# The residual x plus the output's bias, made in DRAM by DMA instead of on GpSimd

## The chip, the core and the metric

The kernel runs on one NeuronCore of a Trainium2 chip. The core has five engines that run their own instruction streams: TensorE (PE; its weight loads are listed as PEld), VectorE (DVE), ScalarE (ACT), GpSimd (POOL) and SyncE (SP, which here only issues DMAs). They wait for each other by semaphores. DMAs issued by SP and by GpSimd run on the same 16 DMA engines; the profile calls SP's queue q1 and GpSimd's q0. SBUF is the memory on the core (128 partitions), PSUM the small memory that TensorE writes into, DRAM the memory off the core.

The metric is the device time of one execution in microseconds; the median of three runs is given.

## The reference

The input x has 4 batches of 1024 tokens with 512 channels, ctx the same shape. One layer of cross attention with 16 heads of 32 channels is followed by a quantised feed-forward net:

```python
x = x + xattn(layernorm(x), ctx, Wq, bq, Wk, bk, Wv, bv, Wo, bo)
x = x + ffn(layernorm(x), clip_x, clip_down, w_gate, w_up, w_down)

# xattn: q from layernorm(x); k and v from ctx
scores = q k^T / sqrt(32), masked:
    # the first 768 tokens, "image", attend within their own third of 256
    # the last 256, "text", attend to all image tokens and causally to text
out = softmax(scores) v @ Wo + bo

# ffn: activations fake-quantised to 8 bits with ONE scale for the whole tensor
xq = round(x / s) * s          # s = sigmoid(clip) * max|x| / 127
h  = fakequant(silu(xq @ Wg^T) * (xq @ Wu^T))
y  = h @ Wd^T
```

The scale s needs the maximum over all tokens, so the feed-forward part cannot begin before the attention is done with every token. The sum x + bo has nothing to do with the attention: it is one number for each element of x and could be made at any time before the attention's output is added to it.

## The kernel before

**Tiles and stages.** The 4096 tokens are cut into 16 blocks of 256; each batch has three image blocks and one text block. The attention stage takes about 880 us, the feed-forward stage the rest. Between them the sum x + attention lies in a DRAM tensor, x1_d (the profile leaves out digits in names and calls it x_d).

**Units.** One unit is a block and a group g of four heads against one key block. An image block has 4 units (its own key block only), a text block 16: four groups with four parts each, one part for each key block of its batch. That makes 112 units. The loop over n, of 118 iterations, runs a software pipeline: iteration n makes the row maxima of unit n (products s, then L450 or L468 on VectorE), the weights of unit n - 5 (T_LAG; products t of L504 and L509, exponentials L514 and L518 on ScalarE) and the values of unit n - 6 (V_LAG; products av, L554). Projections of q, k and v and the output's products (pp_q, pp_kv, pv, po, all at L226) fill TensorE in between, by a table of targets. An iteration takes 5 to 10 us.

**Row sums.** GpSimd adds the exponentials of a unit into sp (L535), twice for most parts of a text unit; in a text block's last part it also clears the upper triangle (L523). TensorE then sums sp by a product with ones (L573), in the values step one iteration later.

**The normalised input.** layernorm(x) of a block is made in three background steps, one for each iteration as they come up: statistics (VectorE, L365), deviation (two small operations on ScalarE, then seven on GpSimd, L373 to L379) and apply (ScalarE, L383). The normalised block goes to DRAM (xn_d) and comes back as spread_q in another order of rows; VectorE transposes it (L267) into the operand of the q projection. The tile xb that holds the block has one buffer, so the next xb is loaded when the write of xn_d has landed. The loads of ctx (spread_kv) take the same way and share spread_q's one buffer. The background is a queue: the deviation at its head holds back what stands behind it, the quantising of the feed-forward weights.

**The bias.** bo_b holds the bias of the output in all 128 partitions; in iterations 2 to 5 the part of bv that passes through Wo is added to it (output_bias; complete at L206).

**The output.** When a block's four groups are done, its xr, a 512 KB block of x, is loaded (L136, two buffers). GpSimd adds bo_b to it (add_bias, L613), one or two iterations after the load is issued. The product po of 128 tokens is added by VectorE (take, L618), which frees po's PSUM bank, the only one that the projections and the outputs share. Statistics for the second layernorm and the token's maximum and minimum follow (L625 to L628), and GpSimd issues the write of the block to x1_d (L631). The last block (tail) is added to its products by TensorE instead.

**What sets the order.** TensorE, VectorE, ScalarE and GpSimd run their instructions in the order in which the program writes them. SP is not in that list: the order of its DMA issues is made by a planner from what is ready when. An engine's instructions, SP's DMA issues too, start in order: one that waits holds up those behind it.

Of the kernel before, what the change touches and what calls it, by code (L numbers as in the profile page):

```python
# [10 lines left out]
F32 = mybir.dt.float32  # L11
# [3 lines left out]
ALU = mybir.AluOpType  # L15
# [4 lines left out]
P = 128  # L20
B, N, C = 4, 1024, 512
NH, D = 16, 32
FF = 1408
NCC = C // P
NIC = FF // P
QB = 256
NQB = N // QB
# [15 lines left out]
def kernel(ctx: ExitStack, tc: tile.TileContext, x, kv, Wq, bq, Wk, bk, Wv, bv, Wo, bo, clip_x, clip_down, w_gate, w_up, w_down, out):  # L43
    nc = tc.nc
    x_tok = x.rearrange("b n c -> (b n) c")
# [7 lines left out]
    x1_d = dram.tile([B * N, C], F32, tag="x1_d", name="x1_d")  # L53
# [68 lines left out]
    with ExitStack() as actx:  # L122
        wk2 = actx.enter_context(tc.tile_pool(name="wk2", bufs=2))
# [4 lines left out]
        ap = actx.enter_context(tc.tile_pool(name="ap", bufs=1))  # L128
# [5 lines left out]
        def load_block(src, c, tag, bufs=1):  # L134
            t = ld.tile([P, 2, C], F32, tag=tag, name=f"{tag}_{c}", bufs=bufs)
            nc.sync.dma_start(t, src[c * QB : (c + 1) * QB, :].rearrange("(t p) c -> p t c", p=P))  # L136
            return t
# [10 lines left out]

        brow = ap.tile([3 * NCC, P], F32, tag="brow", name="brow")
        bqk = ap.tile([P, 3 * NCC], F32, tag="bqk", name="bqk")  # L150
        bo_b = ap.tile([P, C], F32, tag="bo_b", name="bo_b")
        mask = ap.tile([P, P], F32, tag="mask", name="mask")
        NMB = 4
        nm2s = [ap.tile([P, 2, 4, D], BF16, tag=f"nm2_{i}", name=f"nm2_{i}") for i in range(NMB)]
# [18 lines left out]

        def other_loads():
            nc.sync.dma_start(W["Wo"], Wo.rearrange("(c p) f -> p c f", p=P))
            nc.gpsimd.dma_start(bo_b, bo.partition_broadcast(P))
            for name, clip in (("x", clip_x), ("h", clip_down)):
                sig[name] = cpool.tile([P, 1], F32, tag=f"sig_{name}", name=f"sig_{name}")
                nc.gpsimd.dma_start(sig[name], clip.partition_broadcast(P))
# [8 lines left out]
        def output_bias():  # L188

            bvr = wk2.tile([P, NCC, D], F32, tag="wst", name="bvr", bufs=1)  # L190
            parts = wk2.tile([P, C], F32, tag="sp", name="bo_parts")

            def spread():
                nc.vector.memset(bvr, 0.0)
                nc.vector.tensor_copy(bvr[:, :, 0:1], bqk[:, 2 * NCC :].unsqueeze(2))

            def product():
                pb = ps_sc.tile([P, 2, 2, QB], F32, tag="sc", name="pbo").rearrange("p a b c -> p a (b c)")[:, 0, :]
                for cc in range(NCC):
                    nc.tensor.matmul(pb[rows_of(cc)], bvr[:, cc, :], W["Wo"][:, cc, :], start=True, stop=True, tile_position=(0, cc * D), skip_group_check=True)  # L200
                nc.scalar.copy(parts, pb)

            def total():
                pb = ps_sc.tile([P, 2, 2, QB], F32, tag="sc", name="pbt").rearrange("p a b c -> p a (b c)")[:, 0, :]
                nc.tensor.matmul(pb, ones, parts, start=True, stop=True)
                nc.vector.tensor_tensor(bo_b, pb, bo_b, ALU.add)  # L206

            return spread, product, total

# [41 lines left out]
        class Job:  # L251


            def __init__(self, kind, c, a):
                self.kind, self.c, self.a = kind, c, a
                self.small, self.big, self.part = 0, 0, 0
                self.smalls = 2 if c == 0 else 1
                self.bigs = 4 if kind == "kv" else 2
# [93 lines left out]
        background = deque()  # L352
# [54 lines left out]
        def rows_of(j):  # L407
            return slice(j * D, (j + 1) * D)
# [181 lines left out]

                return avs, av, quotient

        at_end = [False]
        later = []

        class Output:


            def __init__(self, k):
                self.k, self.xr, self.i, self.part, self.biased = k, None, 0, 0, False  # L600

            def load(self):
                if self.xr is None:
                    self.xr = load_block(x_tok, self.k.c, "xr", bufs=2)
                    if at_end[0]:
                        later.append(self.add_bias)
                    else:
                        later.append(lambda: later.append(self.add_bias))

            def add_bias(self):  # L610
                if not self.biased:
                    self.biased = True
                    nc.gpsimd.tensor_tensor(self.xr, self.xr, bo_b.unsqueeze(1).to_broadcast([P, 2, C]), ALU.add)  # L613

            def take(self, po, i, cols):
                self.add_bias()
                xr, t0 = self.xr, 2 * self.k.c
                nc.vector.tensor_tensor(xr[:, i, cols], po[:, cols], xr[:, i, cols], ALU.add)  # L618
                if cols.stop < C:
                    return None  # L620
                name = f"st2_{self.k.n}_{i}"

                def statistics():
                    st = small.tile([P, 6], F32, tag="st2", name=name)
                    nc.vector.bn_stats(st, xr[:, i, :])  # L625
                    nc.vector.bn_aggr(mv2[:, t0 + i, :], st)
                    nc.vector.tensor_reduce(xm2[:, t0 + i, 0:1], xr[:, i, :], AX.X, ALU.max)
                    nc.vector.tensor_reduce(xm2[:, t0 + i, 1:2], xr[:, i, :], AX.X, ALU.min)  # L628

                if i == 1:  # L630
                    nc.gpsimd.dma_start(x1_d[t0 * P : (t0 + 2) * P, :].rearrange("(t p) c -> p t c", p=P), xr)  # L631
                return statistics
# [50 lines left out]
        T_LAG, V_LAG = 5, 6  # L683
        units = []
        for b in range(B):
            for qb in range(NQB) if b < B - 1 else (0, TEXT, 1, 2):
                k = Block(b, qb)
# [3 lines left out]
        LATE = len(units) - n_text - 3 * NCC  # L691
# [94 lines left out]
        def step_output(half=False, rests=False):  # L786
            rest = outputs[0].step(half)
            if outputs[0].i == 2:
                outputs.pop(0)

                def take():
                    rest[1]()
                    for o in outputs[:2]:
                        o.load()

                finish((rest[0], take), rests)
            else:
                finish(rest, rests)
# [57 lines left out]
        stage()  # L856
        stage()
        take()
        spent, rows_done["k", 0] = 2 * BIG, NCC
        stage()  # L860
# [9 lines left out]
        send(3)  # L870
        big_step()
        other_loads()
        early[0] = False
        spread, product, total = output_bias()
        for n in range(len(units) + V_LAG):
            at_end[0] = n >= len(units)
            previous = units[n - 1] if 0 < n <= len(units) else None
            if n < len(units):
                u = units[n]
# [6 lines left out]
                    minus_maxima(u)  # L886
            if n in (2, 3, 4, 5):
                (spread, sigmoids, product, total)[n - 2]()
            f = background.popleft() if background and n > 0 else None
            if f is not None and f.__name__ in ("deviation", "apply", "quantise"):  # L890
                f()
                f = background.popleft() if background and f.__name__ == "quantise" else None
# [100 lines left out]
        for i in range(2):  # L993
            t = t0 + i
# [27 lines left out]
    gctx = ExitStack()  # L1022
    f4 = gctx.enter_context(tc.tile_pool(name="f4", bufs=NTT))
    fd = gctx.enter_context(tc.tile_pool(name="fd", bufs=1))
    fd.tile([P, 56], F32, tag="pad", name="pad")

    fx = gctx.enter_context(tc.tile_pool(name="fx", bufs=2))
    xt = load_x1(fx, 0)
# [160 lines left out]
    def steps(h):  # L1189

        return h.rearrange("p i t -> p (i t)").bitcast(BF16).rearrange("p (i u) -> p i u", i=NIC)[:, :, :TB]
# [9 lines left out]
    for n, tb in enumerate(order):  # L1201
        hq, xr = steps(resident[tb]), xrs.pop(tb)
# [74 lines left out]
```

## Time and profile before

| | |
|---|---|
| median of 3 runs | 1130.96 us (1130.71 to 1133.3) |
| the profiled execution | 1132.25 us, of which the span from first to last instruction is 1130.5 us |
| granted TensorE clock, mean | 0.995 |
| TensorE busy | 1106.8 us (98%) |
| VectorE, GpSimd, ScalarE busy | 783.8, 549.0, 502.1 us |
| GpSimd: sums into sp (L535) | 84 and 59 operations, 188.2 and 140.2 us |
| GpSimd: bias adds (L613) | 16 operations, 38.1 us |
| GpSimd: issues of x1_d's writes (L631) | 15, 11.9 us |
| HBM read, written | 71.57 MB, 33.29 MB |

Times are microseconds from the start of the span unless a row says ns. A group's row gives the line, the engine, the operation, what it writes and reads, its shape and number; then busy us and mean ns of one; then how long its engine sat idle before it and what ended that. A row of waits reads "engine line <- whom it waited for: us in total, times, longest". SPq is SP's stream of DMA issues: the duration there is the issue, not the transfer. Matmuls are pipelined, so a busy TensorE need not be at its peak; idle time of an engine that is not the bottleneck costs nothing.

### The profile page before, as it was taken

The page shows a single profiled execution, that of the slowest core. Times are in us where ns is not written, and L with a number is a line of the kernel's source. Part 1 is how long each engine was busy: PE and PEld are TensorE (multiplying, and loading weights), DVE is VectorE, ACT ScalarE, POOL GpSimd, SP SyncE. Part 2 cuts the span into 40 slices and gives each one's busy share as a digit, 9 for nine tenths or more (in the row PEclk, how much of TensorE's full clock was granted, in tenths as well). Part 3 has the DMA queues.
Part 4 walks back from the last instruction along what each step waited for, and adds up shares of the span by engine and source line. Part 5 has one row for each costly group of instructions (what it writes and reads, how often), then busy time and mean ns, then how long its engine had stood idle before and what let it go on. Part 6 is the DMA issues. An engine that isn't in the chain of part 4 may idle for free.

```text
span 1130.5 us, 31464 instructions
## 1 busy us (share of the span) xinstructions
PE 1106.8 (98%) x13829; PEld 553.5 (49%) x13851; DVE 783.8 (69%) x980; ACT 502.1 (44%) x701; POOL 549.0 (49%) x616
## 2 busy tenths in 40 slices
PE   9999999999999999999999999999999899998998
PEld 5545545454445445454544445555544344443444
DVE  2546676766577857567777656876666788877887
ACT  3234444343444434344433345544342465553553
POOL 1224556677754576775646668668753232110110
PEclk9999999999999999999999999999999899999999
DMA  8342223132322231331323123112221599311895
GB/s 261 111 132 65 63 56 96 47 97 76 90 63 76 74 97 43 94 104 36 89 66 88 41 74 86 42 50 63 73 76 47 185 289 253 73 34 33 299 379 191
DMA packets 117201, 119.09 MB, mean 105 GB/s; under 512 B 55548, under 2 KB 86536, under 8 KB 115656
## 3 DMA queue, kind: packets, MB, share of 16 engines
q1 hardware_dynamic: 111104, 83.26, 26.7%
q0 software_dynamic: 5648, 33.30, 7.8%
q8 instruction: 108, 1.77, 0.7%
q10 hardware_dynamic: 312, 0.53, 0.2%
q14 instruction: 29, 0.24, 0.1%
HBM read 71.57 MB, written 33.29 MB: 93 GB/s over the span
## 4 chain that ended last, share of the span: by engine, by line
PE 84%; POOL 7%; DVE 3%; DMA 3%; ACT 2%; issue 1%; POOLq 0%; DVEq 0%; SPq 0%; ACTq 0%
PE pv L226 9%; PE pp_kv L226 8%; PE pp_q L226 8%; PE av L554 8%; PE po L226 8%; PE t L509 7%; PE pg L1117 7%; PE pu L1117 7%; PE s L457 5%; POOL sp L535 4%; PE s L446 4%; PE av L573 3%; PE t L504 3%; PE pd L1220 2%; DMA xt<-x_d 2%
## 5 line engine op out<-in xcount | busy, mean ns | idle before, releaser
L514 ACT ACTIVATE pT<-t 128x1024 f32<-128x1024 f32 x112 | 114.8, 1025 | 332.1 <-PE t L509 310.0
L535 POOL TENSOR_TENSOR sp<-sp,pT 128x1024 f32<-128x1024 f32 x84 | 188.2, 2240 | 45.0 <-ACT pT L518 41.6
L535 POOL TENSOR_TENSOR sp<-pT 128x1024 f32<-128x1024 f32 x59 | 140.2, 2376 | 97.7 <-ACT pT L518 86.7
L468 DVE TENSOR_REDUCE nmh<-s 128x2 f32<-128x1024 f32 (+1 forms) x128 | 145.2, 1157 | 60.1 <-PE s L457 57.9
L450 DVE TENSOR_REDUCE nmh<-s 128x4 f32<-128x1024 f32 x96 | 112.8, 1218 | 84.3 <-PE s L446 84.3
L226 PE MATMUL pv<-Wv_sb,kvT 128*32 128x512 f32 (+1 forms) x1088 | 120.5, 570 | 1.6 <-DVE xr L618 1.6
L226 PE MATMUL pp_q<-qT,Wq_sb 128*32 128x256 f32 x2048 | 121.3, 380 | 0.2
L554 PE MATMUL av<-pT,va 128*32 128x256 f32 (+1 forms) x1792 | 116.9, 377 | 0.0
L226 PE MATMUL po<-Wo_sb,oT 128*32 128x512 f32 (+1 forms) x1120 | 112.2, 534 | 2.7 <-DVE xr L618 2.4
L518 ACT ACTIVATE pT<-t 128x1024 f32<-128x1024 f32 x112 | 114.5, 1023 | 0.0
L509 PE MATMUL t<-qT,kT 32*128 32x256 f32 (+1 forms) x1792 | 113.4, 366 | 0.0
L226 PE MATMUL pp_kv<-kvT,Wk_sb 128*32 128x256 f32 x1920 | 112.5, 380 | 0.1
L588 DVE RECIPROCAL avs<-avs 128x256 f32<-128x256 f32 x63 | 109.7, 1742 | 0.0
L509 PEld LDWEIGHTS t<-qT,kT 32*128 32x128 f32 x1792 | 88.1, 184 | 6.7
L1117 PE MATMUL pg<-xqT,wgT 128*128 128x512 bf16 x344 | 90.0, 381 | 1.1 <-DVE xqT L1078 0.5
L1117 PE MATMUL pu<-xqT,wuT 128*128 128x512 bf16 x345 | 90.2, 382 | 0.4
L589 POOL TENSOR_TENSOR oT<-avs 128x256 f32<-128x256 f32 x63 | 46.2, 734 | 90.1 <-DVE avs L588 89.9
L1123 ACT ACTIVATE silu<-pg,sg 128x512 f32<-128x512 f32 x88 | 60.0, 687 | 65.3 <-PE pg L1117 63.2
L226 PEld LDWEIGHTS pp_q<-qT,Wq_sb 128*32 128x32 f32 x2048 | 63.3, 110 | 48.3 <-issue 5.5
L1144 DVE SCALAR_TENSOR_TENSOR h<-pu,su,silu 128x512 f32<-128x512 f32 x88 | 65.4, 747 | 30.5 <-PE pu L1117 27.8
L226 PEld LDWEIGHTS pp_kv<-kvT,Wk_sb 128*32 128x32 f32 x1920 | 60.2, 110 | 43.6 <-issue 2.3
L554 PEld LDWEIGHTS av<-pT,va 128*32 128x32 f32 x1792 | 47.0, 109 | 53.5 <-issue 30.0
(191 smaller groups left out, 1448.0 us busy)
## 6 DMA issues: line engine op xcount, KB each, us to landing
xt<-x_d SPq DMA_DIRECT2D x16, 1024.0 KB, 6.1
h<-h_d POOLq DMA_DIRECT2D x3, 2816.0 KB, 14.2
xb<-in_x_dram SPq DMA_DIRECT2D x16, 512.0 KB, 3.7
xr<-in_x_dram SPq DMA_DIRECT2D x16, 512.0 KB, 3.6
x_d<-xr POOLq DMA_DIRECT2D x16, 512.0 KB, 3.7
spread_kv<-in_ctx_dram SPq DMA_DIRECT2D x60, 128.0 KB, 2.8
xn_d<-xb SPq DMA_DIRECT2D x15, 512.0 KB, 3.4
spread_q<-xn_d SPq DMA_DIRECT2D x60, 128.0 KB, 2.7
```

Of the source, the lines that this page charges most:

```text
L226: nc.tensor.matmul(out[rows_of(j)], lhs[:, rows_of(j)], rhs, start=start, stop=stop, tile_position=(0, j * D), skip_group_check=True)
L450: nc.vector.tensor_reduce(nmh[:, h, :, :, 0], prs[h], AX.X, ALU.max, negate=True)
L468: nc.vector.tensor_reduce(nmh[:, h, :, i, half], s[:, :, :n], AX.X, ALU.max, negate=True)
L509: nc.tensor.matmul(prs[j // 2][:, j % 2, n, cols], kc[rows_of(j), g, n * P : (n + 1) * P], q[rows_of(j), g, cols], start=False, stop=(n == 1))
L514: nc.scalar.activation(pT[:, :2], prs[0], AF.Exp)
L518: nc.scalar.activation(pT[:, 2:], prs[1], AF.Exp)
L535: nc.gpsimd.tensor_tensor(sp[:, :, cols], a, pT[:, :, n, cols], ALU.add)
L554: nc.tensor.matmul(av[rows_of(j), 0, cols], va[:, n, g * P + j * D : g * P + (j + 1) * D], u.pT[:, j, n, cols], start=(u.part == 0 and n = ...
L588: nc.vector.reciprocal(avs[:, 1, :], avs[:, 1, :])
L1117: nc.tensor.matmul(ps, w[:, cc, ic * P : (ic + 1) * P], qT[:, cc, :], start=(cc == 0), stop=(cc == NCC - 1))
L1123: nc.scalar.activation(s, pg, AF.Silu, scale=sg[:, ic : ic + 1])
L1144: nc.vector.scalar_tensor_tensor(h[:, ic, :], pu, su[:, ic : ic + 1], s, ALU.mult, ALU.mult)
```

## The change

x + bo is made in DRAM, in x1_d itself, early in the attention stage. When bo_b is complete (iteration 5), SP issues four DMAs that write it to every row of x1_d, one DMA for each batch: 128 partitions, eight rows of 2 KB from each, 2 MB. In iterations 7 to 22 GpSimd issues one DMA each that adds 256 rows of x to the same rows of x1_d (a DMA from DRAM to DRAM that accumulates). The block xr is then loaded from x1_d instead of x, with three buffers instead of two, and GpSimd's adds are gone. bo_b itself is loaded by SP instead of GpSimd, and takes one of the three buffers of oT, which hold a block's attention output before Wo; a pad in the feed-forward stage grows by 2 KB for each partition, the difference between the larger xr and the smaller bo_b.

A second change is in the background: while the weights step is at the third or fourth part of a text unit (and before LATE, iteration 84), a deviation at the head of the queue stays there, and nothing is taken from the queue in that iteration.

```diff
-        bo_b = ap.tile([P, C], F32, tag="bo_b", name="bo_b")
+        bo_b = wk2.tile([P, NCC, QB], F32, tag="oT", name="bo_b", bufs=3).rearrange("p a b -> p (a b)")[:, :C]
...
-            nc.gpsimd.dma_start(bo_b, bo.partition_broadcast(P))
+            nc.sync.dma_start(bo_b, bo.partition_broadcast(P))
...
                 nc.vector.tensor_tensor(bo_b, pb, bo_b, ALU.add)
+                for b in range(B):
+                    rows = x1_d[b * N : (b + 1) * N, :].rearrange("(t p) c -> p t c", p=P)
+                    nc.sync.dma_start(rows, bo_b.unsqueeze(1).to_broadcast([P, N // P, C]))
...
             def load(self):
                 if self.xr is None:
-                    self.xr = load_block(x_tok, self.k.c, "xr", bufs=2)
-                    if at_end[0]:
-                        later.append(self.add_bias)
-                    else:
-                        later.append(lambda: later.append(self.add_bias))
-
-            def add_bias(self):
-                if not self.biased:
-                    self.biased = True
-                    nc.gpsimd.tensor_tensor(self.xr, self.xr, bo_b.unsqueeze(1).to_broadcast([P, 2, C]), ALU.add)
+                    self.xr = load_block(x1_d, self.k.c, "xr", bufs=3)
 
             def take(self, po, i, cols):
-                self.add_bias()
                 xr, t0 = self.xr, 2 * self.k.c
...
-            f = background.popleft() if background and n > 0 else None
+            if 7 <= n < 7 + B * NQB:
+                rows = slice((n - 7) * QB, (n - 6) * QB)
+                nc.gpsimd.dma_start(x1_d[rows, :], x_tok[rows, :], accum_op=ALU.add, max_dma_last_dim=C)
+            t = units[n - T_LAG] if T_LAG <= n < LATE else None
+            crowded = t is not None and t.k.text and t.part > 1
+            f = background.popleft() if background and n > 0 and not (crowded and background[0].__name__ == "deviation") else None
...
-    fd.tile([P, 56], F32, tag="pad", name="pad")
+    fd.tile([P, 568], F32, tag="pad", name="pad")
```

More of the change, by code (lines that the diff above doesn't have):

```diff
@@ L591, in values @@
                 return avs, av, quotient
-        at_end = [False]
         later = []
@@ L599, in __init__ @@
             def __init__(self, k):
-                self.k, self.xr, self.i, self.part, self.biased = k, None, 0, 0, False
+                self.k, self.xr, self.i, self.part = k, None, 0, 0
             def load(self):
                 if self.xr is None:
-                    self.xr = load_block(x_tok, self.k.c, "xr", bufs=2)
-                    if at_end[0]:
-                        later.append(self.add_bias)
-                    else:
-                        later.append(lambda: later.append(self.add_bias))
-            def add_bias(self):
-                if not self.biased:
-                    self.biased = True
-                    nc.gpsimd.tensor_tensor(self.xr, self.xr, bo_b.unsqueeze(1).to_broadcast([P, 2, C]), ALU.add)
+                    self.xr = load_block(x1_d, self.k.c, "xr", bufs=3)
             def take(self, po, i, cols):
-                self.add_bias()
                 xr, t0 = self.xr, 2 * self.k.c
@@ L875 @@
         for n in range(len(units) + V_LAG):
-            at_end[0] = n >= len(units)
             previous = units[n - 1] if 0 < n <= len(units) else None
```

## The prediction

> **What bounds the kernel now.** I read the page first, then what TensorE waits for, then the two stretches that the change touches: the first 110 us of the attention loop, and the text groups with the loop's end.
>
> ```profile
> PE 1106.8 (98%) x13829; PEld 553.5 (49%) x13851; DVE 783.8 (69%) x980; ACT 502.1 (44%) x701; POOL 549.0 (49%) x616
> ```
>
> TensorE is busy for 98% of 1130.5 us, so it is the bound. POOL, which the change relieves, is busy for 49%. What POOL's work costs is only what TensorE waits for. The list of TensorE's own waits (total us, times, longest) says how much that is:
>
> ```profile
> PE av L573 <- POOL sp L535: 2.6, 7, 0.7
> PE po L226 <- DVE xr L618: 2.4, 2, 1.8
> ...
> PE pv L226 <- DVE xr L618: 1.6, 2, 0.8
> ```
>
> The last two are the output path: L618 adds a product to xr and frees the only projection bank. The list of all waits puts L618's own lateness on POOL ("DVE xr L618 <- POOL xr L613: 18.0, 4, 6.1"): four times the bias add came late, and TensorE lost 4.0 us. That is all that the bias costs now.
>
> **Part 1: the bias add leaves POOL.** Two groups of the by-form listing price it:
>
> ```profile
> L613 POOL TENSOR_TENSOR xr<-xr,bo_b 128x1024 f32<-128x1024 f32 x16 | 38.1, 2378 | 5.4 <-DMA xr<-in_x_dram 5.3
> ...
> L631 POOL DMA_DIRECT2D x_d<-xr x15 | 11.9, 791 | 16.5 <-DVE xr L618 16.2 <-issue 0.2
> ```
>
> 16 adds of 2378 ns go, 38.1 us of POOL. 16 accumulating DMAs come, issued by POOL. The trace has none; the nearest row is L631, 791 ns to issue 512 KB. From below, the 541 ns of the h_d writes; from above, twice L631, as both sides are rows in DRAM. I take 791: 12.7 us, so POOL is relieved of 25 us. Of that only the waits count. At 305 and 518 us the late add held the next pv by 0.8 us each; at 837 by 0.6; at 855 the add waits for its load, issued at 852.14 because the second xr buffer was in use until L628 at 852.08, and po waits 1.8. The third buffer lets that load go early. Gain **4.0 us**, the sum of the two rows.
>
> **Part 2: factors out of the last text parts.** The factors are seven small POOL operations, 1.8 us from 284.99 to 286.79. They move only where they meet a text unit's third or fourth part; by the times of L373 those at 285, 498 and 648 us do. At 285 the triangle select that follows could have started at 286.2, when the exponentials ended, and starts at 286.75: 0.5 us of the 0.7 us wait at the row-sum product. Twice, as 648 meets no wait behind it: **1.0 us**. The price is a normalised block an iteration or two later (6.7 us each). Its cover is that the load of spread_q at 677.96 waits for a DVE transpose anyway; without cover that block would cost up to 6 us.
>
> **Part 3: the bias written to DRAM through SP's queue.** This is where the time is lost. Once bo_b is complete, four DMAs of 2 MiB each write it to all 4096 rows of x1_d. In time order around there (start, us, engine, operation):
>
> ```profile
> 70.18 0.67 DVE L206 TENSOR_TENSOR bo_b<-pbt,bo_b 128x512 f32<-128x512 f32 x1
> ...
> 75.57 0.38 SPq L385 DMA_DIRECT2D xn_d<-xb  x1
> ...
> 78.37 0.39 SPq L136 DMA_DIRECT2D xb<-in_x_dram  x1
> ...
> 80.21 1.93 SPq L146 DMA_DIRECT2D spread_q<-xn_d  x4
> ...
> 89.17 0.64 DVE L365 BATCH_NORM_STATS2 st<-xb 128x6 f32<-128x512 f32 x1
> ...
> 90.99 2.15 DVE L267 STREAM_TRANSPOSE qT<-spread_q 128x1024 f32<-128x1024 f32 x1 [0.17 <-PE pp_q L226]
> ...
> 93.08 2.31 DVE L450 TENSOR_REDUCE nmh<-s 128x4 f32<-128x1024 f32 x2
> ...
> 95.95 0.40 PE L504 MATMUL t<-nmT,onesb 2*128 2x512 bf16 x4
> ```
>
> The writes go out at 70.85, ahead of the write of xn_d. What follows on SP's queue then waits for their data: small transfers behind large ones on this queue show it. The DMA issues at 7.5 us (behind Wv and Wq) and at 896.5 us (behind a 1 MiB xt), with size and us to landing:
>
> ```profile
> spread_kv<-in_ctx_dram SPq DMA_DIRECT2D x1, 128.0 KB, 10.2
> ...
> xqT<-xq SPq DMA_TRANSPOSE x1, 5.5
> ```
>
> Alone these take 2.4 to 2.8 and 2.4 us. The rate comes from 1041.4 us, where four xt loads of 1 MiB stand on this queue:
>
> ```profile
> xt<-x_d SPq DMA_DIRECT2D x1, 1024.0 KB, 5.6
> ```
>
> The first lands after 5.6 us; while they run the slices show about 395 GB/s, 2.65 us per MiB, so 2.95 us is fixed. Eight MiB: 70.85 + 2.95 + 8 x 2.65 = **95.0 us**. The Trainium skill, "DMA: Bandwidth & Descriptors", section "Anatomy of one DMA", gives 2.0 us plus the bytes at 436 GB/s: 21.2 us, done at 92.1, which would make the stall below 2.9 us shorter. Our row has this queue and 2 KB packets, so I keep 95.0 and the other for the range.
>
> One accumulation is in the way too. POOL issues the first one after nm at 87.96, when the first 2 MiB are down (about 79), so POOL doesn't wait, but its data shares the engines with the end of the writes. By the row, 512 KB is 1.3 us. The Trainium skill, "Collectives: The Full Stack", section on the bandwidth ceiling, says that an adding DMA reads two sources and takes twice a copy's read traffic: an estimate of 2.65 us. No run here shows an accumulation; I take 2.65, with 0 and 5.3 as the ends. By the row alone the stall would be 1.3 us shorter.
>
> The chain from there, each step with its present duration: xn_d is 0.5 MiB, 1.3 us, landed at 95.0 + 2.65 + 1.3 = 99.0. xb cannot load before that (one buffer). From the issue of xb to the last spread_q landing it takes 86.1 - 78.4 = 7.8 us now: 106.8. The statistics of L365 wait in between, from 89.2 on, and VectorE does its work in order, so the transpose (2.15) and the maxima (first half 1.2) come behind: 110.2. The second bank of t's products is one that those maxima free; TensorE needs it at 96.2. **Stall: 14.0 us**, in the ninth iteration. Behind L365 on VectorE stand L267, L450 and L588, and POOL's nm waits for L450, but the stall at TensorE covers these. The transposes of nm behind the writes are used four iterations after their issue (88.7 is due at about 139), so they cost nothing.
>
> After some 3.6 us without products between 1042 and 1046 the granted clock was 0.5 for 3.4 us (0.68 in the window 1045 to 1050). The same after this hole costs half of 3.4: **1.7 us**.
>
> The other pieces cost nothing, by their cover: the 256 KB of bo on SP instead of POOL (0.7 us of queue at 13 us, where two xr loads of 512 KB leave the same queue; without that, 0.7 us); bo_b in one of three oT buffers (third block's oT, iteration 14, after 140 us; without cover, the wait for the writes); the pad (it keeps the later pools where they were); the loads of xr from DRAM rows that were summed long before (first used at 148.7). Accumulations 2 to 16 come one to an iteration of 7 to 10 us and fall on chains with 6 us of slack (spread_q issued at 116.71, its four parts landed by 121, used at 127.02). POOL's issues of iterations 18 to 22 meet text units; 0.8 us there could delay a row sum by as much, four times at most.
>
> **Sum.** -4.0 - 1.0 + 14.0 + 1.7 = +10.7 us. The profiled execution took 1132.25 us (span 1130.5 and 1.75 around it): 1142.95. The median shown is 1.3 lower: 1130.96 + 10.7, about **1141 us** with the small terms rounded down.
>
> **Rivals.** Measurement tells about 0.3%, 3.4 us, from no change.
> - A, the stall as above: 1141. Its own range is 1134 (writes by 92.1, no delay by the accumulation, spread_q ahead of xb: stall 7, gain 5) to 1150 (accumulation 5.3, clock 3.4, gains 3). Chance 0.66.
> - B, the writes are hidden and only the gains stay: 1126. The mechanism is the order on SP, which a planner makes and not the program: if xn_d, xb and spread_q of this iteration are issued ahead of the writes, nothing waits. For no stall the maxima must end by 96.2, so xb must go by 85 and the writes land by 81, 10 us for 8 MiB: twice the rate of the row. So only the order decides. Against it: bo_b is ready at 70.85, xb's normalised values at 75.54. Chance 0.18.
> - C, the order or the rate save most of the stall, and gains and loss cancel: 1128 to 1134. Chance 0.08.
> - D, accumulation is slow: at 8 us each, the first adds 5.4 to the stall, and the later chains lose their 6 us of slack, some 8 us in all: 1155. Chance 0.08.
>
> So faster 0.18, same 0.08, slower 0.74. The range 1126 to 1150 leaves out D, A's top and half of B.
>
> **What would show it.** A hole of 8 to 17 us at TensorE near 96 us, with L365 or L267 on VectorE waiting for xb or spread_q; xn_d issued near 75 landing after some 20 us in place of 2.8; granted clock 0.5 just behind; no L618 waits on POOL, and none at 855. If TensorE has no hole there, part 3 is wrong and B holds. If text groups grow, POOL's issue was mis-sized.

## The result and the profile after

The changed kernel takes 1143.21 us (median of 4 runs, 1142.2 to 1143.8) against 1130.84 us (1130.68 to 1133.3) for the kernel before in the same session. The ratio is 1.0103, with a 95% interval from 1.0086 to 1.0121: **12 us slower**. The profiled execution took 1142.85 us, its span is 1141.1 us, and the granted clock was 0.989 on average (0.995 before).

The busy times on the page barely move, although the kernel is a per cent slower:

```profile
PE 1108.7 (97%) x13829; PEld 554.8 (49%) x13851; DVE 783.8 (69%) x980; ACT 501.7 (44%) x701; POOL 530.7 (47%) x615
```

POOL is relieved of 18.3 us, and TensorE is as busy as before. So the time is idle time, and the list of what TensorE waited for (total, times, longest) says which:

```profile
PE t L507 <- DVE nmh L453: 14.9, 2, 14.6
...
PE av L576 <- POOL sp L538: 1.7, 7, 0.3
```

One wait of 14.6 us is new. The two waits for L618 that the bias add had caused (2.4 and 1.6 us) are gone, and the waits for POOL's sums fell from 2.6 to 1.7. In the list of all waits, nothing waits for GpSimd on the output path any more (the add into xr is L610 now):

```profile
DVE xr L610 <- PE po L229: 32.1, 20, 4.1
POOL x_d L623 <- DVE xr L610: 16.9, 7, 4.2
```

The other side of the trade, in the by-form groups: each accumulating DMA holds GpSimd for 1331 ns, 21.3 us in all, where the adds had taken 38.1.

```profile
L882 POOL DMA_DIRECT2D x_d<-in_x_dram x16 | 21.3, 1331 | 0.1
```

Now SP's stream of issues around the hole (start, duration of the issue, not of the transfer):

```profile
72.26 10.38 SPq L209 DMA_DIRECT2D x_d<-bo_b  x4
82.74 3.36 SPq L388 DMA_DIRECT2D xn_d<-xb  x1
86.21 10.32 SPq L495 DMA_TRANSPOSE nmT<-nm  x2
100.74 1.80 SPq L146 DMA_DIRECT2D spread_q<-xn_d  x4
102.60 0.44 SPq L136 DMA_DIRECT2D xb<-in_x_dram  x1
```

The four writes of the bias stand ahead of xn_d. The first two are issued in 0.38 and 0.58 us, the last two hold SP for 4.30 and 4.99 us. So xn_d leaves at 82.74 in place of 75.57. The transfers by issue (KB, us from issue to landing), for the windows of the last two writes, of xn_d, of the first accumulation and of spread_q:

```profile
x_d<-bo_b SPq DMA_DIRECT2D x4, 2048.0 KB, 18.6
...
xn_d<-xb SPq DMA_DIRECT2D x1, 512.0 KB, 17.9
...
x_d<-in_x_dram POOLq DMA_DIRECT2D x1, 512.0 KB, 14.2
...
spread_q<-xn_d SPq DMA_DIRECT2D x4, 128.0 KB, 3.2
```

The 18.6 us of the first line belong to the third write, the only one of the four whose landing the listing gives. By the semaphores the last of them is down at 98.4, xn_d at 100.7 (82.74 + 17.94), and only then can spread_q and xb go. VectorE's rows and TensorE's, in order of time:

```profile
106.77 0.69 DVE L368 BATCH_NORM_STATS2 st<-xb 128x6 f32<-128x512 f32 x1 [16.84 <-DMA xb<-in_x_dram]
...
108.50 1.99 DVE L270 STREAM_TRANSPOSE qT<-spread_q 128x1024 f32<-128x1024 f32 x1
110.41 2.32 DVE L453 TENSOR_REDUCE nmh<-s 128x4 f32<-128x1024 f32 x2
```

```profile
96.62 0.39 PE L507 MATMUL t<-nmT,onesb 2*128 2x512 bf16 x2
111.65 0.61 PE L507 MATMUL t<-nmT,onesb 2*128 2x512 bf16 x2 [14.64 <-DVE nmh L453]
```

VectorE stands still for 16.84 us until xb lands, and the maxima that free TensorE's bank come behind it. The clock pays as well. By window (length, busy time and instructions of PE, granted clock, DMA share, GB/s):

```profile
100.00:105.00 5.00, 0.00 (x0) 0.69 1.25 192
105.00:110.00 5.00, 0.00 (x0) 0.50 0.60 200
110.00:116.00 6.00, 4.35 (x42) 0.54 0.44 109
116.00:120.00 4.00, 4.00 (x76) 1.00 0.97 119
```

I cut the attention stage into iterations at the first product t and took the TensorE work of each, by its number of products, from its length; what remains is called left over here. Most of the first 80 iterations have 0.62 to 0.66 us left over, in both kernels. The stage ends at 876.34 us before and at 888.38 after: +12.0. Of that, the iteration with the hole gives +16.9 (the hole, and behind it 2.60 us left over in place of 0.64), the start and the sixth iteration +0.7, and everything later gives back 5.5. The feed-forward stage is 1.4 us shorter in this execution, which I leave to the scatter.

### The profile page after: what moved, and what is told of

It reads as the page before. It is cut to its first block, busy times and chain, and to the rows that moved or that the text cites. A ratio compares the mean times of both kernels' runs of the same rounds, so it can differ in the third digit from the quotient of the medians.

```text
span 1141.1 us, 31476 instructions
## 1 busy us (share of the span) xinstructions
PE 1108.7 (97%) x13829; PEld 554.8 (49%) x13851; DVE 783.8 (69%) x980; ACT 501.7 (44%) x701; POOL 530.7 (47%) x615
## 3 DMA queue, kind: packets, MB, share of 16 engines
q0 software_dynamic: 22208, 41.42, 13.7%
HBM read 79.96 MB, written 50.07 MB: 114 GB/s over the span
## 4 chain that ended last, share of the span: by engine, by line
PE 86%; POOL 4%; DVE 3%; DMA 2%; ACT 2%; issue 1%; SPq 0%; POOLq 0%; DVEq 0%; ACTq 0%
PE pv L229 9%; PE po L229 9%; PE av L557 9%; PE pp_q L229 8%; PE pp_kv L229 7%; PE t L512 7%; PE pg L1113 7%; PE pu L1113 7%; PE s L460 5%; PE pd L1216 5%; PE s L449 4%; POOL sp L538 3%; PE av L576 3%; PE t L507 3%; DMA xn_d<-xb 2%
## 5 line engine op out<-in xcount | busy, mean ns | idle before, releaser
L517 ACT ACTIVATE pT<-t 128x1024 f32<-128x1024 f32 x112 | 114.7, 1024 | 333.7 <-PE t L512 310.1
L453 DVE TENSOR_REDUCE nmh<-s 128x4 f32<-128x1024 f32 x96 | 112.7, 1216 | 85.6 <-PE s L449 85.6
## 6 DMA issues: line engine op xcount, KB each, us to landing
x_d<-bo_b SPq DMA_DIRECT2D x4, 2048.0 KB, 18.6
```

Of the source, the lines that this page charges most:

```text
L453: nc.vector.tensor_reduce(nmh[:, h, :, :, 0], prs[h], AX.X, ALU.max, negate=True)
L517: nc.scalar.activation(pT[:, :2], prs[0], AF.Exp)
```

## The experiments

Medians stand against the kernel before in the same session (1131.7 to 1132.5 us). "Hole" is TensorE's longest new wait in the profiled execution.

### Is it the order on SP's queue?

The prediction said that the transfers behind the writes on SP's queue wait for their data. Two runs take the chain and the writes apart.

**The chain on GpSimd.** The one xn_d, xb and spread_q that stood behind the writes are issued by GpSimd.

```diff
-                    nc.sync.dma_start(xn_d[c].rearrange("(t p) c -> p t c", p=P), xb)
+                    (nc.gpsimd if c == 3 else nc.sync).dma_start(xn_d[c].rearrange("(t p) c -> p t c", p=P), xb)
... the same for xb of block 4 and for spread_q of block 3
```

> As the changed kernel, but the three transfers of the late chain (the write of the normalised block 3, the load of the next xb, and the four loads of spread_q for block 3) are issued by GpSimd, so they are no longer behind the 8 MiB on SP's queue. Theory, order on the queue: the hole of 14.6 us at TensorE near 97 us shrinks to 4 us or less and the half clock behind it goes; time 1126 to 1131 us. Rival, the 16 DMA engines are simply full until 98 us whichever queue one uses: the chain is at most a little quicker, a hole of 8 to 14 us stays; 1136 to 1143 us.

Measured: 1139.45 us (1135.19 to 1139.67), ratio 1.0056 (1.0037 to 1.0076). The hole is 8.4 us.

```profile
PE t L507 <- DVE nmh L453: 8.4, 1, 8.4
```

In this execution the order on SP is worth some 6 us of the 14.6. It is the fastest of the four; the other three took 4 us more, and by the ratios (1.0103 and 1.0056) the gain is about 5 us. The rest of the hole stays, although nothing stands ahead of the chain on its queue: its transfers are slow themselves. Issue to landing, on GpSimd's queue:

```profile
xn_d<-xb POOLq DMA_DIRECT2D x1, 512.0 KB, 9.8
...
xb<-in_x_dram POOLq DMA_DIRECT2D x1, 512.0 KB, 9.8
spread_q<-xn_d POOLq DMA_DIRECT2D x1, 128.0 KB, 8.7
```

Before, xn_d took 2.8 us in this chain, and spread_q, issued behind xb, 4.6 (window 81.6 to 81.8 us). Between 95 and 160 us the medians of spread_q and xb were 2.7 and 3.4.

**The writes on GpSimd.** The reverse: SP has the chain and no large write.

```diff
-                    nc.sync.dma_start(rows, bo_b.unsqueeze(1).to_broadcast([P, N // P, C]))
+                    nc.gpsimd.dma_start(rows, bo_b.unsqueeze(1).to_broadcast([P, N // P, C]))
```

> As the changed kernel, but the four 2 MiB writes of the bias are issued by GpSimd; SP's queue carries none of them. Theory, order on the queue: SP's chain runs beside the writes at about half rate, so VectorE's statistics wait no more than 3 us for xb. GpSimd pays for the issues: at 0.8 us for 256 rows, 3.2 us for one write, 13 us in a row from 72 us, and the sums sp that it makes for units 0 and 1 come late; a hole of 4 to 8 us at TensorE near 80 us, for that reason; 1131 to 1137 us. Rival, full engines: the hole near 97 us stays at 8 us or more; 1138 to 1146 us.

Measured: 1143.62 us (1142.92 to 1144.64), ratio 1.0103 (1.0088 to 1.0118): no gain at all. The hole is 16.1 us.

```profile
PE t L507 <- DVE nmh L453: 16.1, 1, 16.1
```

Two things stand behind it. The first is lateness on the way to xn_d. GpSimd's four issues take 0.89 to 1.02 us each, but in a row they hold its deviation and its nm, and on SP a transpose that reads nm stands ahead of xn_d:

```profile
70.89 3.66 POOL L209 DMA_DIRECT2D x_d<-bo_b  x4 [0.29 <-DVE bo_b L206]
```

```profile
71.20 10.05 SPq L495 DMA_TRANSPOSE nmT<-nm  x2
81.34 1.41 SPq L388 DMA_DIRECT2D xn_d<-xb  x1
93.01 4.37 SPq L146 DMA_DIRECT2D spread_q<-xn_d  x4
97.42 1.08 SPq L136 DMA_DIRECT2D xb<-in_x_dram  x1
```

xb is normalised at 77.97 in place of 75.54, and xn_d is issued at 81.34 in place of 75.57. So 5.8 us of the 16.1 are not the transfers' own, and an estimate of what they alone would leave is 10 us, near the 8.4 of the run before. The second is the transfers themselves. DMA from 70.8 to 98 us (queues: packets, MB, share of the 16 engines; then the issues):

```profile
q0 software_dynamic: 2156, 8.36, 87.0%
q1 hardware_dynamic: 919, 0.69, 9.6%
...
x_d<-bo_b POOLq DMA_DIRECT2D x4, 2048.0 KB, 17.9
xn_d<-xb SPq DMA_DIRECT2D x1, 512.0 KB, 11.5
x_d<-in_x_dram POOLq DMA_DIRECT2D x1, 512.0 KB, 18.0
spread_q<-xn_d SPq DMA_DIRECT2D x4, 128.0 KB, 10.1
xb<-in_x_dram SPq DMA_DIRECT2D x1, 512.0 KB, 9.9
```

SP's queue q1 holds nothing but small transfers. Over the window they get a tenth of the engines, though for part of it none of them was issued; once issued, each takes 9.9 to 11.5 us. The records of single packets say how that may come about: between 80 and 95 us GpSimd's packets are of 4096 bytes and take 160 ns each, those of xn_d are of 2048 bytes and take 84 ns, those of spread_q, later, are of 512. If the engines take packets from the queues in turn, the queue with small packets gets the smaller part. That is argued from the sizes; no run here changed the packet size. What is shown by the two runs is that another queue does not keep small transfers quick beside 8 MiB: with either arrangement they take 8 to 11.5 us.

### Is it the burst?

**512 KB in each iteration.** The same 8 MiB go out in 16 writes, issued by ScalarE in iterations 6 to 21; each accumulation comes one iteration after its write, as in the change.

```diff
-                for b in range(B):
-                    rows = x1_d[b * N : (b + 1) * N, :].rearrange("(t p) c -> p t c", p=P)
-                    nc.sync.dma_start(rows, bo_b.unsqueeze(1).to_broadcast([P, N // P, C]))
...
+            if 5 < n <= 5 + B * NQB:
+                rows = x1_d[(n - 6) * QB : (n - 5) * QB, :].rearrange("(t p) c -> p t c", p=P)
+                nc.scalar.dma_start(rows, bo_b.unsqueeze(1).to_broadcast([P, 2, C]))
```

> As the changed kernel, but the bias is written by 16 DMAs of 512 KB, one in each of the iterations 6 to 21, issued by ScalarE; the bytes moved are the same. Theory, order on the queue: no transfer of SP waits behind more than its share of one 512 KB write; no hole near 97 us, full clock, and the gains of the rest (5.5 us between 106 us and the end of the attention stage) stay: 1125 to 1128 us. Rival, the bytes themselves cost (25 MB more through the same engines in the attention stage): 1135 us or more. A third possibility, ScalarE pays for its 16 issues by late exponentials: 1128 to 1133 us with holes behind exponentials.

Measured: 1127.26 us (1125.13 to 1130.55), ratio 0.9961 (0.9946 to 0.9977). Same bytes, same queue for the accumulations, and **faster than the kernel before**. One small hole is left, at 131, with the clock at half behind it from 134.8 to 138.3:

```profile
PE t L504 <- DVE nmh L468: 1.8, 1, 1.8
```

The writes are on another queue here too, ScalarE's. No run put the whole burst on that queue, so its part is not shown alone; the two runs above say that a change of queue leaves 8 us or more.

**512 KB in every second iteration.** Writes in iterations 6, 8, ... 36, accumulations in 7, 9, ... 37, in place of the change's own writes and accumulations.

```diff
+            if n >= 6 and (n - 6) % 2 == 0 and (n - 6) // 2 < B * NQB:
+                c = (n - 6) // 2
+                rows = x1_d[c * QB : (c + 1) * QB, :].rearrange("(t p) c -> p t c", p=P)
+                nc.scalar.dma_start(rows, bo_b.unsqueeze(1).to_broadcast([P, 2, C]))
+            if n >= 7 and (n - 7) % 2 == 0 and (n - 7) // 2 < B * NQB:
+                rows = slice((n - 7) // 2 * QB, ((n - 7) // 2 + 1) * QB)
+                nc.gpsimd.dma_start(x1_d[rows, :], x_tok[rows, :], accum_op=ALU.add, max_dma_last_dim=C)
```

> The bias written in 16 DMAs of 512 KB by ScalarE, one in every second iteration (6, 8, ... 36), and each accumulation one iteration after its write. Same bytes as in the change, 1 MiB of traffic for each 15 us or so in place of 8 MiB at once. Theory (what cost the time is the bytes in one burst beside a chain of three dependent small transfers): no hole near 96 us and none at the thirteenth iteration either, where the writes in every iteration left 1.8 us; the gains of about 5.5 us stay: 1124 to 1127 us. Rival (the writes and accumulations cost something wherever they stand, by issue time on ScalarE and GpSimd): as with a write in every iteration or slower, 1127 to 1131.

Measured: **1124.18 us** (1123.83 to 1126.1), ratio 0.9932 (0.9920 to 0.9944). It beats both kernels. No wait for the maxima is left in TensorE's list, and the longest total in the attention stage is the one for GpSimd's sums:

```profile
PE av L573 <- POOL sp L535: 1.8, 7, 0.4
```

The clock is at 90% or more in every slice of the span, where the changed kernel has a 7 in the fourth:

```profile
PEclk9999999999999999999999999999999999999999
```

Its attention stage ends at 870.76 us, 5.6 us earlier than before: the gains alone. From the run just above it differs in the spacing alone, and its stage ends 3.7 us earlier (874.43 there): the small hole and its clock. The other 3 us of the span (1121.9 against 1130.5) come from the feed-forward stage, where the clock of before fell to 0.5 from about 883 to 889 and this one's did not. The change does not touch that stage. It does not follow the burst either: the profiles with 512 KB in each iteration, in every second one, the same with two buffers, and half the burst have full clock there, but so has the one with the whole burst in iteration 8 below. So these 3 us are not credited to the spreading.

**Half the burst.** The first two writes stay on SP as in the change; the other 4 MiB go out in 512 KB writes by ScalarE in iterations 14 to 21.

```diff
-                for b in range(B):
+                for b in range(B // 2):
...
+            if 14 <= n < 22:
+                rows = x1_d[(n - 6) * QB : (n - 5) * QB, :].rearrange("(t p) c -> p t c", p=P)
+                nc.scalar.dma_start(rows, bo_b.unsqueeze(1).to_broadcast([P, 2, C]))
```

> The change with only the first two of the four writes of 2 MiB in the burst on SP; the other half goes out later, in 512 KB writes by ScalarE in iterations 14 to 21. Theory (the stall is the time of the bytes ahead of and beside the chain): 4 MiB less at 2.65 us each takes 10.6 us off the stall of 14.6: a hole of 2 to 6 us near 96, 1129 to 1134 us. Rival (a stall that does not follow the bytes, such as one fixed delay of the queue behind any large write): the hole stays above 10 us, 1138 to 1143.

Measured: 1131.81 us, ratio 1.0004 (0.9989 to 1.0018), but twelve runs spread from 1127.61 to 1136.19, far wider than any other kernel here. The profile is of the fastest one and shows a hole of 1.2 us. There xn_d lands 9.6 us after its issue at 75.98, that is at 85.6, and the maxima begin at 96.75, just at the need.

```profile
PE t L507 <- DVE nmh L453: 1.2, 1, 1.2
...
xn_d<-xb SPq DMA_DIRECT2D x1, 512.0 KB, 9.6
```

The stall follows the bytes: 13.4 us less in that execution for 4 MiB less, where 10.6 were expected. By the ratios of the medians (1.0103 and 1.0004) this kernel is 11 us faster than the change. What the slower runs of this kernel lost, no profile shows.

**The burst in iteration 8.** The four writes by GpSimd, but from 95.75 us on, and the accumulations three iterations later too, in place of the change's own.

```diff
+            if n == 8:
+                for b in range(B):
+                    rows = x1_d[b * N : (b + 1) * N, :].rearrange("(t p) c -> p t c", p=P)
+                    nc.gpsimd.dma_start(rows, bo_b.unsqueeze(1).to_broadcast([P, N // P, C]))
+            if 10 <= n < 10 + B * NQB:
+                rows = slice((n - 10) * QB, (n - 9) * QB)
```

> The four writes of 2 MiB in one burst as in the change, but issued by GpSimd in iteration 8 (near 96 us) in place of iteration 5, and the accumulations three iterations later too (10 to 25). To be read beside the same writes on GpSimd's queue in iteration 5, which left a hole of 16.1 us. Theory (the burst costs what the dependent small transfers lose beyond their slack): the next chain begins with the write of the normalised block at 104.9 and ends with spread_q, used at 127.0; by the trace of before spread_q is issued at 116.7 and lands by 121, so 6 us of slack. The burst runs from 97 to about 120; the write of the normalised block lands some 9 us later than without it, but the load of spread_q waits for its buffer until 116.7 anyway: 0 to 4 us of hole, 1126 to 1132 us. Rival (8 MiB in one burst costs its 14 us wherever it stands): 1138 to 1143 us.

Measured: 1140.1 us (1138.36 to 1140.51), ratio 1.0073 (1.0056 to 1.0090); the hole is 11.6 us, at 131. My theory missed; the time is in the rival's range. SP's stream shows what I had left out:

```profile
108.26 1.52 SPq L385 DMA_DIRECT2D xn_d<-xb  x1
119.30 0.38 SPq L136 DMA_DIRECT2D xb<-in_x_dram  x1
129.78 0.37 SPq L136 DMA_DIRECT2D xr<-x_d  x1
130.31 2.14 SPq L146 DMA_DIRECT2D spread_q<-xn_d  x4
```

xn_d landed at 119.3 and xb went at once, but the next in the order is xr, which reads what the first accumulation writes. That accumulation was issued at 113.3, into the burst, and landed after 16.4 us, at 129.7. Only then could spread_q go. A dependent load that waits on SP holds up all that stands behind it.

**The same without accumulations.** The sum then lacks x.

```diff
-            if 10 <= n < 10 + B * NQB:
-                rows = slice((n - 10) * QB, (n - 9) * QB)
-                nc.gpsimd.dma_start(x1_d[rows, :], x_tok[rows, :], accum_op=ALU.add, max_dma_last_dim=C)
```

> The burst of 8 MiB in iteration 8 by GpSimd as just before, without the sixteen accumulations (x is left out of the sum, the output lacks it). With them the hole was 11.6 us at 131: the load of xr waited until 129.8 for the first accumulation (issued at 113.3, landed 16.4 us later), and spread_q, which stands behind it on SP, was issued at 130.3. Theory (the burst found slack on this chain, and what was late is SP's order behind the wait for the accumulation): spread_q is issued at about 119.7, behind xb, and lands by 128: a hole of 0 to 3 us, 1126 to 1131 us. Rival (the burst's own traffic costs 8 us or more wherever it stands): the hole stays above 8 us, 1136 to 1141.

Measured: 1134.45 us (1133.21 to 1136.2), ratio 1.0021 (1.0011 to 1.0031); the hole is 6.1 us in the profiled execution, the slowest of the nine, between the two expectations. The planner used the freedom that the edit gave:

```profile
104.46 3.51 SPq L136 DMA_DIRECT2D xr<-x_d  x3
...
111.75 1.47 SPq L385 DMA_DIRECT2D xn_d<-xb  x1
126.66 0.37 SPq L136 DMA_DIRECT2D xb<-in_x_dram  x1
...
128.41 4.10 SPq L146 DMA_DIRECT2D spread_q<-xn_d  x4
```

Three loads of xr, 1.5 MiB more, now stand ahead of xn_d in the burst, and xn_d landed at 126.7, 19 us later than before (104.92 + 2.8 = 107.7). The hole is 6.1, so this chain's slack took 13 us of it. So the price of the burst does depend on the slack where it stands, but the edit did not hold the order still, and how much of the 6.1 is the burst alone stays open.

### The terms of the sum

**The first accumulation's share of the stall.** The change without its accumulations (the sum lacks x).

```diff
-            if 7 <= n < 7 + B * NQB:
-                rows = slice((n - 7) * QB, (n - 6) * QB)
-                nc.gpsimd.dma_start(x1_d[rows, :], x_tok[rows, :], accum_op=ALU.add, max_dma_last_dim=C)
```

> The change without the sixteen accumulating DMAs (x is left out of the sum, the output lacks it). The prediction put 2.65 us of the stall on the data of the first accumulation. By that the hole is 11 to 13 us and the time 1138 to 1141, GpSimd's issue time being gone too. Rival: the accumulation comes too late to delay the chain (it was issued at 88.9, when xn_d was under way, and landed at 103.0, after it): the hole stays at 14 to 15 us, the time at 1141 to 1143.

Measured: 1141.44 us (1141.34 to 1143.03), ratio 1.0090 (1.0075 to 1.0105). The hole is 12.9 us, 1.7 less, as by the prediction's own account; the rival's 14 to 15 is out. The times do not decide: 1141.44 lies just above the first range and in the rival's, and the ratio's interval overlaps the change's.

```profile
PE t L507 <- DVE nmh L453: 12.9, 1, 12.9
...
xn_d<-xb SPq DMA_DIRECT2D x1, 512.0 KB, 15.7
```

Without the accumulation xn_d lands 15.7 us after its issue, in place of 17.9: 2.2 us less. The hole shrinks by less because the planner used the freedom here too: an xr load of 512 KB, which no longer waits for an accumulation, goes out at 93.96, ahead of spread_q. So 1.7 is the net of both.

**The clock behind the hole.** 64 products of a constant into the bank of av keep TensorE going through the hole; the result is not used.

```diff
+            if n == 8:
+                warm = ps_av.tile([P, 2, QB], F32, tag="av", name="warm")
+                for _ in range(64):
+                    nc.tensor.matmul(warm.rearrange("p a (b c) -> p (a b) c", b=2), onesb, rhs, start=True, stop=True)
```

> As the changed kernel, with 64 products of 512 columns into an unused bank (13.8 us at full clock) put into TensorE's order where its hole begins, in iteration 8. Theory, the hole costs twice, once by its length and once by the half clock that TensorE is granted behind it (from 101.9 to 115.6 us, of which some 4 us carry work): the products keep the clock at full, and the time falls by about 2 us to 1141 us. Rival, the clock behind the hole costs nothing because TensorE waits anyway: 1143 us, no change.

Measured: 1142.15 us (1139.07 to 1144.1), ratio 1.0087 (1.0068 to 1.0105). The window behind the hole ran at full clock, where the change had 0.54:

```profile
110.00:116.00 6.00, 4.66 (x77) 1.00 0.36 94
```

From the second half of the products t to the next iteration it now takes 9.86 us (111.84 to 121.70), where the change took 11.72 (111.65 to 123.37). The attention stage ends at 886.59, 1.8 us earlier than in the changed kernel's profile. The medians differ by 1.1 us and their intervals overlap, so the profile, not the times, sizes the clock at about 2 us.

**The factors alone.** The kernel before with only the second part of the change.

```diff
+            t = units[n - T_LAG] if T_LAG <= n < LATE else None
+            crowded = t is not None and t.k.text and t.part > 1
+            f = background.popleft() if background and n > 0 and not (crowded and background[0].__name__ == "deviation") else None
```

> The kernel before with the second part alone: the deviation kept out of the third and fourth parts of a text unit. The prediction: 1.0 us faster (0.5 us at 285 and at 498 us each), 1129 to 1131 us. Rival: nothing, as the triangle select and the sums take the time elsewhere: within 0.3 us; or slower by up to 6 us, if a normalised block comes late.

Measured: 1131.25 us over 22 runs, ratio 0.9989 (0.9983 to 0.9996): 1.2 us faster, between 0.5 and 1.9. The iterations at 288.5 and 501.4 us have 1.06 us left over in place of 1.56, and no other up to the end of the loop changes by 0.1. The row of the waits says the same (2.6 before):

```profile
PE av L573 <- POOL sp L535: 1.7, 7, 0.3
```

**The third buffer.** The best version (writes in every second iteration) with two xr buffers and a spare tile.

```diff
+        spare = ld.tile([P, 2, C], F32, tag="spare", name="spare")
...
-                    self.xr = load_block(x1_d, self.k.c, "xr", bufs=3)
+                    self.xr = load_block(x1_d, self.k.c, "xr", bufs=2)
```

> The same with two buffers for xr in place of three (a spare tile keeps the addresses). It prices the third buffer. Theory of the prediction: the third buffer is worth the 1.8 to 2.0 us of the wait at the loop's end (near 850 us), since the block that is loaded there could not go earlier with two: 1.5 to 2.5 us slower than with three. Rival: with GpSimd's adds gone, two buffers do as well, since the load needs about 2.5 us and the add behind it is what was late: within 0.5 us of it.

Measured: 1124.83 us (1123.94 to 1126.94), ratio 0.9939 (0.9928 to 0.9951), which overlaps the 0.9932 with three. VectorE does wait for the late load:

```profile
DVE xr L609 <- DMA xr<-x_d: 3.8, 1, 3.8
```

But TensorE does not: the iteration there has 0.27 us left over with two buffers and with three, against 2.27 before. The third buffer is worth nothing that can be measured.

## Why the prediction came out right, and where its reasons did not

The forecast was 1141 us and slower; 1143.2 was measured. By its own steps:

- **The waits of the output path, 4.0 us.** Held in size. The iterations at 303, 516, 837 and 854 us lost 0.85, 0.85, 0.8 and 2.0 us of what they had left over, 4.5 in all. The reason given for the last one failed: "The third buffer lets that load go early". With two buffers the load is still late, and harmless, since GpSimd's add of 2.4 us behind it is gone.
- **The factors, 1.0 us.** Held, in both places named.
- **The stall, 14.0 us.** 14.6 measured, but as a sum of errors of both signs, so that it came so near is partly luck. The last write landed at 98.4, not 95.0 (+3.4): the writes went out at 72.3 (70.85 was taken) and took 26.2 us for 8 MiB, in which xn_d and others had a share. The row from this trace, with 24.2, was nearer than the estimate of 21.2 us by the Trainium skill, "DMA: Bandwidth & Descriptors", section "Anatomy of one DMA"; that fit is given for GpSimd's path, and these writes were SP's. xn_d landed 2.2 us behind the last write, not 3.95 (-1.7). From there to the last landing it took 6.1 us, not 7.8 (-1.7), because the planner put spread_q ahead of xb; the possibility was named under rival A, not taken. That order has a price which the prediction leaves out: xb landed last, so VectorE's statistics stood on the path, and from the last landing to TensorE it took 4.9 us, not 3.4 (+1.5). TensorE needed the bank at 97.0, not 96.2 (-0.8). The accumulation, taken at 2.65, cost xn_d 2.2 us and the hole 1.7 net.
- **The reason for the stall.** The step "what follows on SP's queue then waits for their data" fits the changed kernel: xn_d landed 2.2 us behind the last write. It is only part of the cause. Another queue for the chain saved about 6 us of the hole and left 8.4; the writes on another queue left 16.1, some 10 of them by the transfers. What failed is the conclusion under rival B, "So only the order decides", which made an order ahead of the writes a full escape, with a chance of 0.18. What the runs show beside the order is a saturated resource: 16 engines, busy throughout at 370 to 390 GB/s (80 to 95 us, with the writes on SP's and on GpSimd's queue), for 26 us. Beside it, in the two runs that take chain and writes apart, each transfer of the chain took 8 to 11.5 us, where it had taken 2.8 to 4.8. The cure is the one that the prediction did not weigh: the same bytes, spread out.
- **The clock, 1.7 us.** About 2.0 by what is left over behind the hole (2.60 against 0.64), 1.9 by the same stretch in the run with TensorE kept busy (9.86 us against 11.72).
- **GpSimd's issue, 791 ns.** Mis-sized: 1331 ns, so 21.3 us and not 12.7, and POOL is relieved of 18.3 us, not 25. No wait of TensorE comes of it.
- **Accumulations 2 to 16 cost nothing.** Held: behind the iteration with the hole, no iteration is longer than its counterpart of before by more than 0.03 us. Rival D, 8 us for each, did not come.

The sum was +10.7; by the medians it is +12.4, by the attention stage 16.9 + 0.7 - 5.5 = +12.0. The gap to the latter is 0.9 us on the hole (14.9 with the products that stand alone ahead of it), 0.3 on the clock and 0.7 on the start and the iteration of the writes, less 0.5 more gain.

## What to carry to other kernels

A transfer that nothing on the critical path waits for still costs what the small dependent transfers beside it lose: find the chain with the least slack in the time that the bulk needs at the measured rate, and if the slack is less, spread the bulk in pieces over iterations before looking for another queue. A load that waits for data on an in-order issue stream is a wait for all that stands behind it, so look at what a planner puts there. And when a sum comes out right, undo its terms one by one: here the size was right and the main reason only a part of it.

## What the runs showed of the hardware that I had not expected

- **An accumulating DMA moves in small packets.** In the packet records, an accumulation of 512 KB goes out as 1024 packets of 512 bytes at 64 ns, where the plain write of xn_d has 256 packets of 2048 bytes at 84 ns. GpSimd's queue took 13.7% of the 16 engines in the changed kernel and 7.8% without the accumulations: 5.9% of 1141.1 us over 16 of them is 4.2 us of all engines each, about three times the 1.3 us of a plain 512 KB. Their median landing is 6.6 us. Whether the packet size follows from the accumulation or from the last dimension that the kernel asks for (max_dma_last_dim) was not tried. The doubled read traffic that the prediction took from the Trainium skill ("Collectives: The Full Stack", on the bandwidth ceiling), which says it of the adds of a ReduceScatter, does not show in the profile's count of HBM traffic: with the accumulations it reads 8.39 MB more and writes 8.39 MB more (79.96 against 71.57, 50.07 against 41.68), once the size of x each. That count is made from the instructions, so it does not settle how often the engines read.
- **SP is held in the issue of a DMA when much is outstanding.** With two writes of 2 MiB under way, the next two issues took 4.30 and 4.99 us and that of xn_d 3.36, where 0.4 is usual. GpSimd's issues of the same writes took 0.9 to 1.0 us each, and with them outstanding SP, without a large write on its own queue, still took 1.41 us to issue xn_d and 1.08 for xb.
